# Selective scan of a four-layer sequence kernel: readout through TensorE turns, one scan per state, du*B on GpSimd

## The chip, the cores and the metric

The kernel runs on one core of one Trainium2 chip. The core's engines that matter here are TensorE (PE; its weight loads are shown apart as PEld), VectorE (DVE), ScalarE (ACT), GpSimd (POOL) and SyncE (SP, which issues the DMAs). Each engine works through its own instructions in a fixed order and waits for others by semaphores. SBUF is the working memory; PSUM is the memory that TensorE writes; the kernel lays it out as eight banks of 128 x 512 float32. The metric is device time in microseconds, the median of repeated runs. All tensors here are float32 unless said otherwise.

## The reference: what is computed

A batch of 32 sequences, each 256 tokens by 256 features, passes through four layers: L0 (linear attention with a gated output), L1 (softmax attention with 16 heads), L2 (a two-way selective state-space layer, E = 512 channels, N = 16 states) and L3 (linear attention, 8 heads). The change lies in L2. For each direction, with u the projected input:

```python
dbc = einsum('bse,re->bsr', u, Wdbc)
dlt, Bm, Cm = split(dbc, [R, R + N])
delta = softplus(einsum('bsr,er->bse', dlt, Wdt) + bdt)
A = -exp(Alog)
dA = exp(delta[..., None] * A)
dBu = delta[..., None] * Bm[:, :, None, :] * u[..., None]
def step(h, xs):
    h = dA_t * h + dBu_t
    y = einsum('ben,bn->be', h, C_t)
...
return ys + u * Dp
```

So for each of 512 channels and 16 states there is a recurrence over 256 tokens, and the 16 states are then weighted by C (which depends on token and state alone) and summed. The second direction runs over reversed time. The two results are added, multiplied by silu of another projection (`act_mx`), projected back to 256 features and added to the residual with a gate.

## The kernel before, in words

After a preamble that folds the weights, everything is recorded into a `Plan` (class at L108) and written out by `place` (L217). `place` is a list scheduler: it simulates the engines with the costs that `_cost` (L176) gives for each operation, hands out the buffers named in `_BUFFERS` and `_BANKS` (L37 and L48) one after the other, and picks the operation that can start first, with ties settled by program order less a head start called `rush` (L288). Its picks become each engine's instruction order; nothing is reordered afterwards. Because all recorded operations are issued at L342, the profile shows L342 for nearly everything, and groups are told apart by the names of their tiles. Where the planner sees TensorE idle for over 0.7 us it inserts filler matmuls (L302 to L317; tiles `g<-w_wf,ident`). It takes SBUF-only VectorE operations and GpSimd operations as excluding each other (`_locks`, L207). The helper `together` (L128) records several matmuls as one operation with the sum of their costs.

One batch's work is `front` (L0, L1 and the first part of L2; L965), `project` for two directions (L998), `act_of` (L1034), four calls of `scan` (L1053), and `back` (L1114: the projection back and L3). In the main loop at L1138 the next batch's front and the last batch's back are woven between the steps of `scan`. So a steady stretch of the program repeats once per batch.

`scan(b, d, cp)` works on one direction d and one half cp of the channels: two blocks (c) of 128 channels on the partitions, 256 tokens along the free axis. `du` (delta times u) is made in PSUM (L1058 to L1065). Then, for each of 8 pairs of states (L1076):

- SP broadcasts the pair's rows of B (`bb`) and C (`cc`) from a DRAM tile `cd` to all partitions, 256 KB each;
- ScalarE makes `dA` = exp(delta*A), four instructions of 255 tokens, into SBUF; a zero column before each segment starts the recurrence anew;
- VectorE multiplies `dbu` = du*B, 128x1024, into two PSUM banks (L1090);
- VectorE scans all four segments (2 blocks x 2 states) in one instruction of 1024 elements into `h` (L1096, L1098);
- GpSimd multiplies `h` by `cc` in place (128x1024, L1102) and adds the pair's two states (128x512, L1105);
- TensorE adds the sum to the running output `yp` in PSUM by a matmul with the identity (128x512, L1108).

`yp` began with the u*Dp projection (L1066 to L1074). At the end of direction 1, VectorE multiplies `yp` with `act` (L1112). Channels lie on the partitions throughout, as `back` needs for its projection (`tok_proj` with `act` as the stationary operand).

In all there are 32 x 4 x 8 = 1024 such steps, 32 per batch. PSUM holds `dbu` (2 banks), `du` (1), `yp` (1) and four general banks `g`.

Of the kernel before, what the change touches and what calls it, by code (L numbers as in the profile page):

```python
# [28 lines left out]
for _n, _w in _COLS:  # L29
# [8 lines left out]
    ("x", 1, [P, 2, D]), ("x1", 1, [P, 2, D]), ("x2", 2, [P, 2, D]), ("xs", 1, [P, 2, D]), ("gate", 2, [P, D]),  # L38
    ("xT2", 2, [P, 2, S]), ("dl", 6, [P, 2, S]), ("dbc", 2, [R + 1 + 2 * N, S]),
    ("bb", 3, [P, 2, S]), ("cc", 4, [P, 2, S]), ("dA", 3, [P, 1025]), ("h", 4, [P, 2, 2, S]), ("act", 4, [P, 2, S]),  # L40
    ("qa", 1, [P, 4, S]), ("ka", 1, [P, 4, S]), ("va", 1, [P, 2, 16, 32]), ("ex", 4, [P, 2, S]), ("mT", 1, [16, S]),
# [5 lines left out]
]  # L47
_BANKS = [("dbu", 1, [P, 2, 2, S]), ("du", 1, [P, 2, S]), ("yp", 1, [P, 2, S]), ("g", 4, [P, 512])]  # L48
_IN_BANKS = {name for name, _, _ in _BANKS}

_RUSH = {"du": 500}


_ADDED = (0, 1, 2, 3, 4, 5, 6, 7)
_SPARE = 0.7
# [52 lines left out]
class Plan:  # L108
# [3 lines left out]
    def __init__(self, nc):  # L112
        self.nc = nc
        self.buffers, self.ops, self.filler = {}, [], None
        for name in ("tensor", "vector", "scalar", "gpsimd", "sync"):
            setattr(self, name, Engine(self, name))
# [10 lines left out]

    def together(self, calls, engine="tensor", method="matmul"):  # L128

        self.add(engine, method, [v for args, _ in calls for v in args], {}, calls)  # L130

    def add(self, engine, method, args, kw, calls=None):
        op = Op()
# [17 lines left out]
        if calls:  # L151
            op.cost = sum(_cost(engine, method, views[3 * i : 3 * i + 3])[0] for i in range(len(calls)))
            if engine == "scalar":

                op.cost += 2.5
        op.rush = max(_RUSH.get(v.tile.name, 0) if w else 0 for v, w in views if isinstance(v, View))
        op.locks = _locks(engine, method, views)
# [18 lines left out]
def _cost(engine, method, views):  # L176

    tiles = [(v, w) for v, w in views if isinstance(v, View)]
    n = max([_elements(v) for v, w in tiles if w] or [0])
    if engine == "sync":  # L180
        return 0.06, 2.6
    if engine == "tensor":
        if method == "transpose":
            return 0.3, 0.2
        w = views[1][0]
        if (w.ap if isinstance(w, View) else w).dtype == BF16:
            return max(0.15, 0.17 + n / 2350), 0.2

        if w.shape[0] <= 32:
            return 0.2, 0.2  # L190
        if w.shape[1] <= 32:
            return 0.23, 0.2
        return max(0.27, 0.06 + n / 570), 0.2
    if engine == "scalar":
        ptr = sum(1 for v, _ in views if not isinstance(v, (View, float, int)) and getattr(v, "shape", (0, 0))[1:] == (1,))
        return 0.2 + n / 1400 + 0.05 * ptr, 0.1
    n = max(_elements(v) for v, _ in tiles)
    if engine == "gpsimd":
        if method == "tensor_tensor":
            return (0.7 if n < 8 else 0.12 + n * 0.00223), 0.1  # L200
        return 0.2 + n / 1000, 0.1
    if method == "tensor_tensor_scan":
        return 0.15 + n / 480, 0.08
    return 0.1 + n / 940, 0.08

# [141 lines left out]
def cond_seq_kernel(ctx: ExitStack, tc: tile.TileContext, a: dict, out: bass.AP):  # L347
# [12 lines left out]
    def load(name, shape, src, eng=None, pool=None, **kw):  # L360
        t = (pool or const).tile(shape, kw.pop("dtype", F32), name=name, **kw)
        (eng or nc.sync).dma_start(out=t, in_=src)
        return t
# [20 lines left out]
    wfo = wtile("wf", 4, 256)  # L384
    blocks = load("blocks", [P, 2, P], a["blocks"])
    w0 = {n: wtile(n + "0", 2, 256) for n in ("wk", "wv", "wq")}
    w3 = {n: wtile(n + "3", 2, 256) for n in ("wk", "wv", "wq")}
# [268 lines left out]

    for t in q.buffers["dA"]:
        nc.gpsimd.memset(t[:, 0:1025:256], 0.0)
    for t in q.buffers["va"]:
# [198 lines left out]
    def attention(ch, x, b, dst):  # L858
# [31 lines left out]
        for h2 in range(8):  # L890
# [3 lines left out]
            for t in range(2):  # L894
                for i in range(2):
# [4 lines left out]
                    ))  # L900
            q.together(calls)
            for i in range(2):
# [13 lines left out]
        for g2 in range(2):  # L916
            av = None
            for h4 in range(4):
# [3 lines left out]
                for m in range(2):  # L922
                    for i in range(2):
# [4 lines left out]
                        ))  # L928
                q.together(calls)
                exs = [q.tile("ex") for _ in range(2)]  # L930
# [5 lines left out]
                for m in range(2):  # L936
                    for i in range(2):
# [7 lines left out]
                        ))  # L945
                q.together(calls)
                yield
# [50 lines left out]
    def project(b, d):  # L998
# [9 lines left out]
        cd = q.tile("cd")  # L1008
        q.sync.dma_start(out=cd, in_=dbc[R + 1 :, :])
        yield  # L1010

# [18 lines left out]
        yield  # L1030
        state[b][d] = (cd, dl)
        yield

    def act_of(b):  # L1034

        xT = state[b]["xT"]
        act = [q.tile("act") for _ in range(2)]
        for e2 in range(2):
            ps = bank()
            for j in range(2):  # L1040
                e = 2 * e2 + j
                for k in range(2):
                    q.tensor.matmul(
                        ps[:, j * 256 : (j + 1) * 256], wx[:, k, e * P : (e + 1) * P], xT[:, k, :],
                        start=k == 0, stop=k == 1,
                    )
            dst = flat(act[e2])
            q.scalar.activation(dst, ps, AF.Tanh, bias=0.0, scale=0.5)
            q.vector.scalar_tensor_tensor(dst, dst, 1.0, ps, ALU.add, ALU.mult)
            yield  # L1050
        state[b]["act"] = act

    def scan(b, d, cp):  # L1053

        s = state[b]
        cd, dl = s[d]
        dl = dl[cp]
        du = q.tile("du")  # L1058
        for c in range(2):
            e = 2 * cp + c  # L1060
            for k in range(2):
                q.tensor.matmul(
                    du[:, c, :], wcz[d][:, k, e * P : (e + 1) * P], s["xT"][:, k, :], start=k == 0, stop=k == 1
                )
        q.vector.tensor_tensor(du, du, dl, ALU.mult)  # L1065
        if d == 0:  # L1066
            s["yp"] = yp = q.tile("yp")
            for c in range(2):
                e = 2 * cp + c
                for k in range(2):  # L1070
                    q.tensor.matmul(
                        yp[:, c, :], wdp[:, k, e * P : (e + 1) * P], s["xT"][:, k, :],
                        start=c == 0 and k == 0, stop=False,
                    )  # L1074
        yp = s["yp"]
        for k in range(N // 2):  # L1076
            n = slice(2 * k, 2 * k + 2)
            bb, cc = q.tile("bb"), q.tile("cc")
            q.sync.dma_start(out=bb, in_=cd[N + 2 * k : N + 2 * k + 2, :].partition_broadcast(P))
            q.sync.dma_start(out=cc, in_=cd[n, :].partition_broadcast(P))  # L1080
            dA = q.tile("dA")
            for c in range(2):
                for j in range(2):
                    o = (2 * c + j) * S + 1
                    q.scalar.activation(
                        dA[:, o : o + S - 1], dl[:, c, 1 - d : S - d], AF.Exp, bias=0.0,
                        scale=aneg[d][:, 2 * cp + c, 2 * k + j : 2 * k + j + 1],
                    )
            dbu = q.tile("dbu")
            q.vector.tensor_tensor(  # L1090
                dbu, du.unsqueeze(2).to_broadcast([P, 2, 2, S]), bb.unsqueeze(1).to_broadcast([P, 2, 2, S]), ALU.mult
            )
            h = q.tile("h")
            hf, uf = h.rearrange("p c n s -> p (c n s)"), dbu.rearrange("p c n s -> p (c n s)")
            if d == 0:
                q.vector.tensor_tensor_scan(hf, dA[:, 0:1024], uf, 0.0, ALU.mult, ALU.add)  # L1096
            else:
                q.vector.tensor_tensor_scan(  # L1098
                    hf[:, ::-1], dA[:, 1:1025][:, ::-1], uf[:, ::-1], 0.0, ALU.mult, ALU.add
                )  # L1100
            hn = h.rearrange("p c n s -> p c (n s)")
            q.gpsimd.tensor_tensor(hn, hn, flat(cc).unsqueeze(1).to_broadcast([P, 2, 2 * S]), ALU.mult)  # L1102
            last = d == 1 and k == N // 2 - 1
            if k in _ADDED:
                q.gpsimd.tensor_tensor(h[:, :, 0, :], h[:, :, 0, :], h[:, :, 1, :], ALU.add)  # L1105
            else:
                q.tensor.matmul(yp, ident, h[:, :, 1, :], start=False, stop=False)
            q.tensor.matmul(yp, ident, h[:, :, 0, :], start=False, stop=last)  # L1108
            yield
        if d == 1:  # L1110
            y = s["act"][cp]
            q.vector.tensor_tensor(y, yp, y, ALU.mult)  # L1112

    def back(b):  # L1114

        s = state.pop(b)
        ps = tok_proj(s["act"], wfo, 2, nk=4)
        x3 = q.tile("x3")
# [122 lines left out]
```

## Time and profile before

| What | Value |
|---|---|
| median of 3 runs | 5332.26 us (5331.7 to 5333.14) |
| profiled execution: span | 5331.4 us |
| mean granted TensorE clock | 0.943 |
| busy: PE, PEld | 4592.1 us (86%), 2963.3 us (56%) |
| busy: DVE | 4786.2 us (90%) |
| busy: ACT | 2940.9 us (55%) |
| busy: POOL | 4419.3 us (83%) |
| DMA | 574.36 MB, mean 108 GB/s |
| first scan starts, last scan ends | 249.6 us, 5291.3 us |

The span is that of one execution, from its first to its last instruction; it stands 0.9 us under the median of the runs. The first 250 us are the weight preamble and the first batch's front; from then on the scans of one batch follow those of the last at a steady pace until 5291 us, and the last batch's back takes the final 40 us. A row of a group reads: line, engine, operation, written tile <- read tiles, shapes, count | busy us in all, mean ns of one | idle time of the engine before it and what ended it. A float32 matmul shows as two records, so counts of matmuls are twice those in the code, except for turns (`g<-ident,...`, transposes by a matmul against the identity), which show as one. In a matmul's row `a*b` is rows times columns of the stationary operand.

### The profile page before, as it was taken

The page shows a single profiled execution, that of the slowest core. Times are in us where ns is not written, and L with a number is a line of the kernel's source. Part 1 is how long each engine was busy: PE and PEld are TensorE (multiplying, and loading weights), DVE is VectorE, ACT ScalarE, POOL GpSimd, SP SyncE. Part 2 cuts the span into 40 slices and gives each one's busy share as a digit, 9 for nine tenths or more (in the row PEclk, how much of TensorE's full clock was granted, in tenths as well). Part 3 has the DMA queues.
Part 4 walks back from the last instruction along what each step waited for, and adds up shares of the span by engine and source line. Part 5 has one row for each costly group of instructions (what it writes and reads, how often), then busy time and mean ns, then how long its engine had stood idle before and what let it go on. Part 6 is the DMA issues. An engine that isn't in the chain of part 4 may idle for free. (4 is left out here: it accounts for less than half of the span.)

```text
span 5331.4 us, 65606 instructions
## 1 busy us (share of the span) xinstructions
PE 4592.1 (86%) x20746; PEld 2963.3 (56%) x20746; DVE 4786.2 (90%) x5047; ACT 2940.9 (55%) x6465; POOL 4419.3 (83%) x3487
## 2 busy tenths in 40 slices
PE   6888888888888888888888888888888888888887
PEld 4655555555555555555555555555555555555555
DVE  2399999999999999999999999999999999999997
ACT  1355565555555565656555656555555555555553
POOL 0288898888898888889888889888889888889887
PEclk7899999999999999999999999999999999999999
DMA  3033333333333333333333334333333333333333
GB/s 100 30 115 109 108 116 107 113 111 109 109 113 111 108 112 111 109 109 114 109 111 107 113 106 117 109 112 110 109 109 115 108 111 111 108 110 114 108 112 88
DMA packets 327816, 574.36 MB, mean 108 GB/s; under 512 B 38214, under 2 KB 61066, under 8 KB 327467
## 3 DMA queue, kind: packets, MB, share of 16 engines
q1 hardware_dynamic: 320466, 562.78, 36.1%
q10 hardware_dynamic: 7002, 7.39, 0.4%
q8 instruction: 163, 2.67, 0.2%
q14 instruction: 185, 1.52, 0.1%
HBM read 558.98 MB, written 10.52 MB: 107 GB/s over the span
## 5 line engine op out<-in xcount | busy, mean ns | idle before, releaser
L342 POOL TENSOR_TENSOR h<-h,cc 128x1024 f32<-128x1024 f32 x1024 | 2416.2, 2360 | 502.9 <-issue 384.2
L342 ACT ACTIVATE dA<-dl,alog 128x255 f32<-128x255 f32 x4096 | 1762.0, 499 | 1269.1 <-DVE h L342 1208.2
L342 DVE TENSOR_TENSOR_SCAN h<-dA,dbu 128x1024 f32<-128x1024 f32 x1024 | 2337.8, 2283 | 131.3 <-PE yp L342 33.8
L342 POOL TENSOR_TENSOR h<-h 128x512 f32<-128x512 f32 x1024 | 1301.4, 1271 | 60.8
L342 PE MATMUL yp<-h,ident 128*128 128x512 f32 x2048 | 1154.4, 652 | 201.7 <-POOL h L342 196.5
L342 DVE TENSOR_TENSOR dbu<-du,bb 128x1024 f32<-128x1024 f32 x1024 | 1255.1, 1226 | 20.0
L342 PEld LDWEIGHTS yp<-h,ident 128*128 128x128 f32 x2048 | 344.1, 198 | 511.2 <-POOL h L342 403.6
L342 PE MATMUL g<-w_wf,ident 128*128 128x256 f32 x1756 | 420.8, 382 | 13.6 <-DVE wf L342 13.1
L342 PEld LDWEIGHTS g<-w_wf,ident 128*128 128x128 f32 x1756 | 329.2, 191 | 140.1 <-issue 43.9
L342 ACT ACTIVATE ex<-g 128x512 f32<-128x512 f32 x512 | 273.8, 595 | 147.4 <-PE g L342 139.5
L342 DVE TENSOR_REDUCE mx<-g 128x2 f32<-128x512 f32 x512 | 319.5, 681 | 22.6 <-PE g L342 16.5
L342 PE MATMUL g<-ka,qa 17*128 17x256 f32 x2048 | 334.9, 454 | 1.7 <-DVE mx L342 1.7
L342 PEld LDWEIGHTS g<-ka,qa 17*128 17x128 f32 x2048 | 225.1, 206 | 132.4 <-DVE mx L342 36.5
L342 PE MATMUL g<-ex,va 128*32 128x256 f32 x2048 | 254.4, 386 | 21.0 <-ACT ex L342 21.0
L342 PE MATMUL du<-xT,w_wcz 128*128 128x256 f32 x1024 | 252.0, 389 | 17.1 <-DVE dbu L342 16.3
L342 PE MATMUL g<-ident,wf 128*128 128x128 f32 x768 | 140.2, 292 | 135.7 <-POOL wf L342 132.4
L342 PE MATMUL g<-qa,ka 18*128 18x256 f32 x2048 | 254.7, 401 | 0.7 <-ACT ex L342 0.7
L342 PEld LDWEIGHTS g<-qa,ka 18*128 18x128 f32 x2048 | 155.2, 184 | 145.4 <-issue 112.3
L342 PEld LDWEIGHTS du<-xT,w_wcz 128*128 128x128 f32 x1024 | 188.9, 192 | 72.0 <-DVE dbu L342 35.7
L342 PEld LDWEIGHTS g<-ident,wf 128*128 128x128 f32 x768 | 91.1, 143 | 229.3 <-POOL wf L342 193.2
L342 PE MATMUL yp<-xT,w_wdp 128*128 128x256 f32 x512 | 195.7, 549 | 24.7 <-DVE act L342 24.6
L342 PE MATMUL g<-wf,w_wk 128*128 128x256 f32 x768 | 206.7, 425 | 1.5 <-ACT wf L342 1.4
(236 smaller groups left out, 6232.3 us busy)
## 6 DMA issues: line engine op xcount, KB each, us to landing
bb<-cd SPq DMA_DIRECT2D x1024, 256.0 KB
cc<-cd SPq DMA_DIRECT2D x1024, 256.0 KB
x<-in_x_dram SPq DMA_DIRECT2D x32, 256.0 KB
out_dram<-xo SPq DMA_DIRECT2D x32, 256.0 KB
fw<-in_film_dram SPq DMA_DIRECT2D x3, 1024.0 KB
rwc<-in_wc_dram ACTq DMA_DIRECT2D x2, 1024.0 KB
qa<-mT SPq DMA_DIRECT2D x128, 4.0 KB
cd<-dbc SPq DMA_DIRECT2D x64, 32.0 KB
```

What stands on the lines that cost most here:

```text
L342: getattr(getattr(nc, op.engine), op.name)(*[real(v) for v in args], **{k: real(v) for k, v in kw.items()})
```

## The change

The recurrence and the sums are the same, but the work is cut and laid out differently. Per batch there are still 32 steps; a step is now one block of 128 channels and four states n = 4x + g (x = 0..3) for a fixed g.

- `bb` holds four rows of B (512 KB); `cc` is gone. `du` moves to SBUF (its matmul goes to a `g` bank, `zp`), and GpSimd makes `dbu` = du*B, 128x1024, in SBUF.
- ScalarE writes exp(delta*A) into PSUM, two states (128x512) to a bank; there are two such banks. Each exp has 256 tokens now.
- VectorE runs one scan of 256 elements per state: first operand in PSUM, second in SBUF, result in SBUF with the states innermost (`h` is [128, 256 tokens, 4 states], so a scan writes every fourth float).
- TensorE turns `h` by eight 128x128 transposes into two `g` banks: the partitions become 32 tokens x 4 states, the free axis channels. ScalarE copies each bank (128x512) into `hT`.
- After two blocks c, eight matmuls with stationary operands of 128x32 (`cm`: C on a diagonal pattern that sums the four states of each token) and 256 moving columns add into `yp`, four of them side by side in the four column groups of 32, recorded with `together`. `yp` and `act` have tokens on the partitions now; `act_of` is written accordingly, and `back` turns `act` back with eight transposes and two copies.
- `cm` is made once per `project`: a DMA reads C back from `cd`, GpSimd reorders it, TensorE turns it, ScalarE copies it, and GpSimd expands it (128x1024).
- PSUM: `dA` 2 banks, `yp` 1, `g` 5. The planner's costs are new too: a transpose 0.112 us (0.3 before), float32 matmuls, ScalarE and VectorE entries changed by little, `together` takes a `share` that divides its cost, and `rush` is 400 for the operations that make `du`.

```diff
-    ("bb", 3, [P, 2, S]), ("cc", 4, [P, 2, S]), ("dA", 3, [P, 1025]), ("h", 4, [P, 2, 2, S]), ("act", 4, [P, 2, S]),
+    ("cm", 3, [P, 32, 32]), ("bb", 3, [P, 4, S]), ("dbu", 2, [P, 4, S]), ("h", 2, [P, S, 4]), ("hT", 3, [P, 4, 2, P]),
+    ("du", 2, [P, 2, S]), ("act", 2, [P, 2, E]),
...
-_BANKS = [("dbu", 1, [P, 2, 2, S]), ("du", 1, [P, 2, S]), ("yp", 1, [P, 2, S]), ("g", 4, [P, 512])]
+_BANKS = [("dA", 2, [P, 2, S]), ("yp", 1, [P, 2, S]), ("g", 5, [P, 512])]
...
         if method == "transpose":
-            return 0.3, 0.2
+            return 0.112, 0.25
...
+        return max(0.22, 0.01 + n / 600), 0.25
...
+        cr, cp, ct, cm = (q.tile(n) for n in ("cr", "cp", "ct", "cm"))
+        q.sync.dma_start(out=cr, in_=cd[0:N, :].rearrange("(x g) (q s) -> (g q) x s", x=4, s=32))
+        q.gpsimd.tensor_copy(cp, cr.rearrange("p x s -> p s x"))
+        ps = bank()
+        q.tensor.transpose(ps[:, :32], cp.rearrange("p s x -> p (s x)"), ident[:32, :32])
+        q.scalar.copy(ct, ps[:, :32])
+        q.gpsimd.tensor_tensor(
+            cm, fours.unsqueeze(1).to_broadcast([P, 32, 32]), ct.unsqueeze(2).to_broadcast([P, 32, 32]), ALU.mult
+        )
...
+        for g in range(4):
+            bb = q.tile("bb")
+            q.sync.dma_start(out=bb, in_=cd[N + g : 2 * N : 4, :].partition_broadcast(P))
+            hT = [q.tile("hT") for _ in range(2)]
+            for c in range(2):
+                dbu, h = q.tile("dbu"), q.tile("h")
+                q.gpsimd.tensor_tensor(dbu, du[:, c : c + 1, :].to_broadcast([P, 4, S]), bb, ALU.mult)
+                for m in range(2):
+                    dA = q.tile("dA")
+                    for j in range(2):
+                        n = 4 * (2 * m + j) + g
+                        q.scalar.activation(
+                            dA[:, j, :], dl[:, c, :], AF.Exp, bias=0.0, scale=aneg[d][:, 2 * cp + c, n : n + 1]
+                        )
+                    for j in range(2):
+                        hv, av, uv = h[:, :, 2 * m + j], dA[:, j, :], dbu[:, 2 * m + j, :]
+                        if d == 1:
+                            hv, av, uv = (v[:, ::-1] for v in (hv, av, uv))
+                        q.vector.tensor_tensor_scan(hv, av, uv, 0.0, ALU.mult, ALU.add)
+                for t in range(2):
+                    ps = bank()
+                    for i in range(4):
+                        q.tensor.transpose(
+                            ps[:, i * P : (i + 1) * P], flat(h)[:, (4 * t + i) * P : (4 * t + i + 1) * P], ident
+                        )
+                    q.scalar.copy(hT[t][:, :, c, :], ps.rearrange("p (i e) -> p i e", i=4))
+                yield
+            for t in range(2):
+                calls = []
+                for i in range(4):
+                    calls.append((
+                        (yp[32 * i : 32 * i + 32, t, :], cm[:, 8 * g + 4 * t + i, :], flat(hT[t][:, i])),
+                        {"start": False, "stop": d == 1 and g == 3 and t == 1},
+                    ))
+                q.together(calls, share=4)
...
+                    q.tensor.transpose(ps[:, o : o + P], act[:, t, e * P : (e + 1) * P], ident)
+            yt.append(copy_of(ps, work("b", e2)))
```

## The prediction

> **What bounds the kernel now.** First the page's busy table, then one long steady stretch in the windows view, because the first 250 us (preamble, first front) and the last 40 us hold no scans.
>
> ```profile
> PE 4592.1 (86%) x20746; PEld 2963.3 (56%) x20746; DVE 4786.2 (90%) x5047; ACT 2940.9 (55%) x6465; POOL 4419.3 (83%) x3487
> ```
> ```profile
> core 0: us, PE busy (x) PEld busy (x) DVE busy (x) ACT busy (x) POOL busy (x), PEclk, DMA share, GB/s
> 1035.00:4052.00 3017.00, 2627.42 (x11933) 1685.70 (x11934) 2819.18 (x2928) 1737.01 (x3822) 2620.09 (x2054) 0.95 0.38 110
> ```
>
> That stretch runs from the first scan of one batch to that of another 19 batches later. Per batch the busy times are DVE 148.4, POOL 137.9, PE 138.3, ACT 91.4 us. The scans of the 32nd batch begin at 5162.4, so a batch takes (5162.4 - 249.6) / 31 = 158.5 us: 1.068 times DVE's work. VectorE bounds it, POOL is next. The waits say the same: ScalarE spends its idle time waiting for VectorE.
>
> ```profile
> ACT dA L342 <- DVE h L342: 1208.2, 612, 7.2
> ```
>
> (Who waits for whom: us, times, longest.) So the change is costed per batch on each engine; the largest sum times 1.068 is the new period.
>
> The rows that price it, from the groups (whole run, then two of the steady stretch):
>
> ```profile
> L342 POOL TENSOR_TENSOR h<-h,cc 128x1024 f32<-128x1024 f32 x1024 | 2416.2, 2360 | 502.9 <-issue 384.2 <-PE yp L342 78.5 <-DVE h L342 28.1
> L342 DVE TENSOR_TENSOR_SCAN h<-dA,dbu 128x1024 f32<-128x1024 f32 x1024 | 2337.8, 2283 | 131.3 <-PE yp L342 33.8 <-PE g L342 3.9 <-ACT dA L342 2.4
> L342 POOL TENSOR_TENSOR h<-h 128x512 f32<-128x512 f32 x1024 | 1301.4, 1271 | 60.8
> L342 DVE TENSOR_TENSOR dbu<-du,bb 128x1024 f32<-128x1024 f32 x1024 | 1255.1, 1226 | 20.0
> ...
> L342 DVE TENSOR_TENSOR du<-du,dl 128x512 f32<-128x512 f32 x128 | 88.3, 690 | 19.5 <-PE du L342 16.6
> ...
> L342 ACT COPY wf<-g 128x512 f32<-128x512 f32 x192 | 112.9, 588 | 133.7 <-PE g L342 133.7
> ```
> ```profile
> L342 PE MATMUL yp<-h,ident 128*128 128x512 f32 x1217 | 684.4, 650 | 106.8 <-POOL h L342 103.4
> L342 PE MATMUL g<-w_wf,ident 128*128 128x256 f32 x874 | 209.3, 381 | 8.3 <-DVE wf L342 8.3
> ```
>
> And from the timeline (start, length, ...), for what one instruction costs when the next follows closely:
>
> ```profile
> 2501.25 0.69 DVE L342 TENSOR_TENSOR du<-du,dl 128x512 f32<-128x512 f32 x1
> 2501.85 0.68 DVE L342 TENSOR_TENSOR wf<-g,qm 128x512 f32<-128x512 f32 x1
> 2502.45 1.22 DVE L342 TENSOR_TENSOR dbu<-du,bb 128x1024 f32<-128x1024 f32 x1
> ...
> 2503.09 0.75 PEld L342 LDWEIGHTS g<-ident,wf 128*128 128x128 f32 x7 [0.42 <-POOL wf L342]
> 2503.58 0.68 DVE L342 TENSOR_REDUCE km<-g 128x2 f32<-128x512 f32 x1
> ...
> 2509.18 2.29 DVE L342 TENSOR_TENSOR_SCAN h<-dA,dbu 128x1024 f32<-128x1024 f32 x1
> ```
> ```profile
> 2089.32 1.13 PE L342 MATMUL g<-qa,ka 18*128 18x256 f32 x8
> 2090.38 1.06 PE L342 MATMUL g<-ex,va 128*32 128x256 f32 x8
> 2091.37 1.13 PE L342 MATMUL yp<-h,ident 128*128 128x512 f32 x2
> ```
>
> **VectorE.** Gone: 32 products and 32 long scans. Neighbours on VectorE overlap by 0.08 to 0.09 us (0.69 long, the next 0.60 later; dbu 1.22, the next 1.13 later), so a product takes 1.14 and a scan 2.20 us: 32 x 3.34 = 106.9. Added: 128 scans of 256. The products of 512 and 1024 elements (690, 1226 ns) give 1.047 ns per element and 154 ns fixed; with the same fixed part the scan runs at (2283 - 154) / 1024 = 2.079 ns per element, so 256 take 532 + 154 = 686 ns, and 0.606 us with the overlap. 128 x 0.606 = 77.6 (87.8 with no overlap, 68.1 with no fixed part). Sum 148.4 - 106.9 + 77.6 = **119** us, ends 110 and 129.
>
> No row shows a scan that writes every fourth float. I take the same pace: the scan already spends two elements' time (2 x 1.047) on each, room for a slower store. [...]
>
> **ScalarE.** The exps stay: 128, one token longer. Into PSUM instead of SBUF: between -4 us (the nearest pair, tanh into PSUM 602 and exp into SBUF 631 ns, on 128) and nothing; I take nothing. Added: 64 copies of 128x512 out of PSUM. Alone 588 ns; two such exps of 595 in a row take 1.08 us, so 0.485 each in a row. 64 x 0.485 = 31.0 (37.6 alone), plus two copies in `back` and two small ones, 1.8. Sum 91.4 + 32.8 = **124** us, ends 120 and 131.
>
> **GpSimd.** dbu has the form of the h*cc product it replaces, 2360 ns. The add goes, 1301.4 / 32 = 40.7. `cm` adds two products of 2.36 and two copies under 0.6 (half-size scalings take 571). 137.9 - 40.7 + 5.9 = **103** us.
>
> **TensorE.** Gone: yp, 684.4 / 19 = 36.0, and fillers, 209.3 / 19 = 11.0 (with PE loaded the planner has no gaps to fill). Left: 91.3. Added:
> - 256 turns. Seven loads for turns take 0.75 us, 0.107 each: 27.4. Were each group of four alone, at the 0.60 us that four took with their tail, 38.4.
> - 128 matmuls of 128x32 in 32 groups of four. The ex,va group is the same shape, four matmuls (eight records), but two column groups: the next matmul starts 0.99 us later. Four side by side need half, 0.50, at best; if only two run at once, 0.99. I take 0.50, since the two groups of a step pair follow each other and share the change of shape: 16.0, end 31.7.
> - eight turns in `back`, 0.9.
>
> Sum 91.3 + 27.4 + 16.0 + 0.9 = **136** us, ends 136 and 162. It may fall to 130 where the 91.3 holds tails that denser work covers (a lone turn counts 0.29 us, not 0.107).
>
> [...] The trace grants 0.95 with 54 turns per batch. At half clock the added turns would cost 55 and the sum 163.
>
> **DMA and SP.** `cc` goes and `bb` doubles, half the bytes at a share of 0.38: no bound. The C read-back waits on SP until `cd` has landed, with `bb` loads queued behind; SP's longest wait for that landing in the stretch was 1.1 us, 64 x 1.1 = 70 us at worst. Three `bb` buffers, two steps each, hide it; so nothing.
>
> **New waits.** Turns wait for the last of a step's four scans; all of PE's queue stands behind them, and `hT`, the C matmuls and the layers' matmuls wait for that. ScalarE's copies wait for the turns, with the next exps behind them; only two `dA` banks (1.2 us of scans each) shield VectorE. The planner's order decides how often. I price this by the old ratio 1.068, for want of a nearer row.
>
> **Sum.** TensorE becomes the bound: 135.6 x 1.068 = 144.8 us per batch. 249.6 + 31 x 144.8 + 128.9 x 144.8 / 158.5 (the last batch's scans) + 40 = 4896 us of span. Adding the 0.9 us by which the span lies under the median: **4897 us**, 8.2% faster. With unknown costs at their gentle and harsh ends but groups four wide, PE is 130 to 147, the time 4710 to 5280.
>
> **Rivals.**
> - *Easy packing (0.12).* TensorE's tails vanish (130) and ScalarE's 124 binds as much; ratio near 1.0: 130 per batch, 4430 to 4720. For it: PE's rows are full of tails. Against: in-order queues coupled in a ring.
> - *The shallow buffers bind (0.15).* Three engines within 15% of each other, with two `dA` banks and two `h`, reach 85% where one bound engine reached 94%: 135.6 / 0.85 = 160, 5370; at 0.88, 154, 5190. So 5190 to 5340, about no gain. For it: ScalarE works in blocks (1.08 us for a pair of attention exps, log tables between). Against: the planner knows these costs.
> - *Slower: the column groups run two at a time (0.11).* Price 0.49 us for each of 32 groups, PE 151.3, period 161.6, time about 5430. Decides from PE x 1.068 = 158.5, that is PE 148.4, or 0.90 us per group. For it: the trace shows no four at once. Against: it shows two at once without loss.
> - *Slower: the strided store (0.05).* If a scan takes two more element times for each token, 0.53 us each, VectorE has 187 us and the time is some 6600. Decides at VectorE 148.4, 0.84 us per scan.
>
> The forecast itself has 0.57, for 4720 to 5190.
>
> **Chances.** Differences under 0.2% (11 us) can't be told from no change. Slower: 0.11 + 0.05 and 0.02 of the shallow buffers, 0.18; same 0.02; faster 0.80. The range 4500 to 5350 leaves out the last two rivals and the edge of the first.
>
> **What would show it.** Right: the period near 145; scans near 0.61 us apart and 690 ns long; turns at 0.11 us in a row; a C group in 0.5 us; copies 485 to 590 ns; PE the engine with least idle time. Wrong: C groups near 1 us, scans over 0.84, a granted clock under 0.9, or VectorE idle behind `dA` with TensorE idle too (the shallow buffers).

## The result, and the profile after

The changed kernel takes 5691.9 us (median of 4 runs, 5671.1 to 5716.8), the one before 5332.7 us in the same session: a ratio of 1.0675, 95% interval 1.0642 to 1.0707. It is slower by 359 us; I had predicted 4897.

The page of the changed kernel first: the busy table, then groups (busy us in all, mean ns of one | idle time before them and what ended it). The line number is now L335.

```profile
PE 5052.0 (89%) x34310; PEld 3563.2 (62%) x34310; DVE 3750.0 (66%) x7096; ACT 4101.7 (72%) x8641; POOL 3297.3 (58%) x2588
...
L335 POOL TENSOR_TENSOR dbu<-du,bb 128x1024 f32<-128x1024 f32 x1024 | 2420.0, 2370 | 1303.5 <-DVE h L335 686.7
L335 DVE TENSOR_TENSOR_SCAN h<-dA,dbu 128x256 f32<-128x256 f32 x4096 | 2537.8, 674 | 945.3 <-ACT dA L335 443.2
L335 ACT ACTIVATE dA<-dl,alog 128x256 f32<-128x256 f32 x4096 | 1924.7, 480 | 418.0 <-DVE h L335 356.5
L335 PE MATMUL g<-ident,h 128*128 128x128 f32 x8192 | 1206.1, 286 | 234.4 <-DVE h L335 189.9
L335 ACT COPY hT<-g 128x512 f32<-128x512 f32 x2048 | 1106.7, 586 | 410.5 <-PE g L335 396.4
...
L335 PE MATMUL yp<-hT,cm 128*32 128x256 f32 x8192 | 618.3, 402 | 68.1 <-ACT hT L335 65.3
...
L335 PE MATMUL g<-w_wf,ident 128*128 128x256 f32 x920 | 242.6, 395 | 0.8 <-ACT hT L335 0.5
```

Three of the four engines have about the work that I had costed; TensorE has more. In the steady stretch (all batches but the first and the last) a batch holds 116.0 us of VectorE (predicted 119), 127.7 of ScalarE (124), 102.8 of GpSimd (103) and 153.1 of TensorE (136). But the first scans of two batches are 170.8 us apart in the mean (predicted 144.8). Over a whole batch no engine is busy for more than nine tenths of the period, and all of them stand in each other's idle columns: VectorE waits for ScalarE's exps, ScalarE for VectorE's scans and TensorE's turns, TensorE for scans, GpSimd for scans. The waits view (who waits for whom: us, times, longest) shows the same ring:

```profile
POOL dbu L335 <- DVE h L335: 686.7, 293, 13.0
...
DVE h L335 <- ACT dA L335: 443.2, 443, 4.6
ACT hT L335 <- PE g L335: 396.4, 250, 9.2
ACT dA L335 <- DVE h L335: 356.5, 348, 6.2
...
DVE h L335 <- PE g L335: 255.0, 33, 8.5
```

The last line, where the trace names a turn as what released the scan, is the wait that two `h` buffers make: a scan may not write into `h` until the turns have read it. There are 33 of them, up to 8.5 us each; in nearly every batch it is one wait of about 8.2 us, ahead of the 15th of the 32 steps.

The windows view, one batch per row from first scan to first scan, shows something else. The columns are the busy times of the engines, then the granted clock of TensorE.

```profile
core 0: us, PE busy (x) PEld busy (x) DVE busy (x) ACT busy (x) POOL busy (x), PEclk, DMA share, GB/s
...
1100.03:1280.20 180.17, 161.54 (x1056) 111.93 (x1055) 115.96 (x218) 127.70 (x270) 102.76 (x81) 0.90 0.20 51
1280.20:1447.93 167.73, 149.13 (x1056) 105.30 (x1055) 115.90 (x218) 127.73 (x270) 102.83 (x81) 0.97 0.22 55
```

The same instructions in the same order take 180.2 us in one batch and 167.7 in the next. Only TensorE's busy time differs, with its clock. The clock records hold spells at half clock in multiples of 3.4 us, 601 us in all after the first 260 us; a line through the batches (all but the first and the last) gives 163.0 us plus 0.44 us for each us at half clock (correlation 1.00; 18.8 us per batch in the mean, from 7 to 41). Below, "at full clock" is the intercept of such a line for the kernel at hand: the period that it gives for a batch with no half clock. For the kernel before it is 154.6 us (0.26 us per us, correlation 0.72, 16.4 us per batch); that line is loose, because its batches all hold between 14 and 21 us of half clock.

The means over a batch also hide that its parts have different limits. Here is the second of these two batches cut further, first its steps 9 to 14, then its last eleven steps:

```profile
1319.44:1374.15 54.71, 53.74 (x377) 35.96 (x376) 29.09 (x57) 32.05 (x67) 18.06 (x12) 0.94 0.17 45
1410.74:1447.93 37.19, 32.38 (x254) 23.95 (x251) 30.60 (x52) 34.11 (x77) 29.34 (x16) 0.97 0.35 86
```

The next batch's softmax attention (scores, exps, `ex,va`) lies in the first of the two. There TensorE is busy for 53.7 of 54.7 us and is the bound by itself, and the long wait for turns falls at its end. In the last eleven steps ScalarE is busiest, at 0.92.

### The profile page after: what moved, and what is told of

The parts are those of the page before. It is cut to its first block, busy times and chain, and to the rows that moved or that the text cites. A ratio compares the mean times of both kernels' runs of the same rounds, so it can differ in the third digit from the quotient of the medians.

```text
span 5701.4 us, 92620 instructions
## 1 busy us (share of the span) xinstructions
PE 5052.0 (89%) x34310; PEld 3563.2 (62%) x34310; DVE 3750.0 (66%) x7096; ACT 4101.7 (72%) x8641; POOL 3297.3 (58%) x2588
## 5 line engine op out<-in xcount | busy, mean ns | idle before, releaser
L335 POOL TENSOR_TENSOR dbu<-du,bb 128x1024 f32<-128x1024 f32 x1024 | 2420.0, 2370 | 1303.5 <-DVE h L335 686.7
L335 DVE TENSOR_TENSOR_SCAN h<-dA,dbu 128x256 f32<-128x256 f32 x4096 | 2537.8, 674 | 945.3 <-ACT dA L335 443.2
L335 ACT ACTIVATE dA<-dl,alog 128x256 f32<-128x256 f32 x4096 | 1924.7, 480 | 418.0 <-DVE h L335 356.5
L335 PE MATMUL g<-ident,h 128*128 128x128 f32 x8192 | 1206.1, 286 | 234.4 <-DVE h L335 189.9
L335 ACT COPY hT<-g 128x512 f32<-128x512 f32 x2048 | 1106.7, 586 | 410.5 <-PE g L335 396.4
L335 PEld LDWEIGHTS g<-ident,h 128*128 128x128 f32 x8192 | 952.7, 146 | 569.9 <-DVE h L335 273.9
L335 PE MATMUL yp<-hT,cm 128*32 128x256 f32 x8192 | 618.3, 402 | 68.1 <-ACT hT L335 65.3
L335 DVE TENSOR_REDUCE mx<-g 128x2 f32<-128x512 f32 x512 | 323.3, 686 | 271.5 <-PE g L335 271.2
L335 POOL TENSOR_SCALAR rs<-mv 128x2 f32<-128x2 f32 x256 | 57.4, 224 | 762.7 <-DVE mv L335 757.3
L335 ACT ACTIVATE ex<-g 128x512 f32<-128x512 f32 x512 | 277.7, 594 | 264.8 <-PE g L335 257.1
L335 PEld LDWEIGHTS yp<-hT,cm 128*32 128x32 f32 x8192 | 181.7, 110 | 354.4 <-ACT hT L335 210.8
L335 PE MATMUL g<-ka,qa 17*128 17x256 f32 x2048 | 326.3, 463 | 2.8 <-DVE mx L335 0.5
L335 PE MATMUL g<-qa,ka 18*128 18x256 f32 x2048 | 318.3, 437 | 0.3 <-ACT ex L335 0.3
L335 PE MATMUL g<-ex,va 128*32 128x256 f32 x2048 | 293.7, 416 | 0.0
L335 PEld LDWEIGHTS g<-ka,qa 17*128 17x128 f32 x2048 | 201.4, 212 | 110.1 <-DVE mx L335 61.0
L335 PEld LDWEIGHTS g<-qa,ka 18*128 18x128 f32 x2048 | 189.9, 202 | 125.2 <-issue 97.8
L335 PE MATMUL g<-xT,w_wcz 128*128 128x256 f32 x1024 | 255.2, 394 | 1.6 <-ACT hT L335 1.6
L335 PE MATMUL g<-w_wf,ident 128*128 128x256 f32 x920 | 242.6, 395 | 0.8 <-ACT hT L335 0.5
L335 PEld LDWEIGHTS g<-xT,w_wcz 128*128 128x128 f32 x1024 | 197.0, 200 | 41.1 <-issue 14.7
L335 PEld LDWEIGHTS g<-w_wf,ident 128*128 128x128 f32 x920 | 168.8, 193 | 61.6 <-issue 26.0
L335 POOL TENSOR_TENSOR rs<-rs,nhalf 128x2 f32<-128x2 f32 x256 | 181.8, 710 | 18.8
L335 PEld LDWEIGHTS g<-ex,va 128*32 128x32 f32 x2048 | 102.0, 115 | 134.4 <-issue 77.4
```

Source lines behind the costliest of these rows:

```text
L335: getattr(getattr(nc, op.engine), op.name)(*[real(v) for v in args], **{k: real(v) for k, v in kw.items()})
```

## Experiments

Two theories at the start. **A**: TensorE, busy 153 of 171 us, is the bound all through the batch. **B**: the engines are tied into a ring by two `h` and two `dA` buffers, so that the fixed order can't absorb any delay. All kernels start from the changed one; ratios are to the kernel before.

| Run | us (median) | ratio, 95% interval | half clock, us | period | at full clock |
|---|---|---|---|---|---|
| changed kernel | 5691.9 | 1.0675 (1.0642 to 1.0707) | 601 | 170.8 | 163.0 |
| e1 no fillers | 5690.3 | 1.0666 (1.0650 to 1.0682) | 834 | 170.3 | 161.8 |
| e2 C cut | 5521.4 | 1.0360 (1.0340 to 1.0380) | 617 | 165.3 | 160.5 |
| e3 exps cut | 5416.3 | 1.0152 (1.0135 to 1.0169) | 378 | 162.5 | 157.3 |
| e4 four `h` | 5255.3 | 0.9858 (0.9823 to 0.9894) | 392 | 157.6 | 152.3 |
| e5 control | 5479.6 | 1.0279 (1.0264 to 1.0295) | 205 | 164.1 | 162.0 |
| e6 four `h`, C cut | 5336.3 | 1.0011 (1.0002 to 1.0021) | 989 | 159.3 | 149.0 |
| e7 four `h`, exps cut | 5160.5 | 0.9687 (0.9645 to 0.9728) | 332 | 153.6 | 149.1 |
| e8 `dA` in SBUF | 6652.8 | 1.2472 (1.2453 to 1.2491) | 1560 | 200.8 | 191.7 |
| e9 eight extra matmuls | 5632.4 | 1.0562 (1.0546 to 1.0578) | 143 | 168.7 | 167.3 |
| e10 four `h`, eight extra | 5331.6 | 0.9999 (0.9989 to 1.0008) | 146 | 159.1 | 157.6 |
| e11 scans cut | 5457.8 | 1.0227 (1.0210 to 1.0244) | 371 | 163.6 | 158.4 |
| e12 three `h` | 5434.4 | 1.0190 (1.0145 to 1.0235) | 485 | 162.6 | 156.0 |
| e13 four `h`, one extra | 5185.0 | 0.9720 (0.9704 to 0.9737) | 156 | 154.4 | 152.3 |
| e14 four `h`, two extra | 5215.1 | 0.9777 (0.9762 to 0.9791) | 174 | 155.2 | 152.9 |
| e15 four `h`, three `dA` | 5474.1 | 1.0265 (1.0244 to 1.0286) | 570 | 163.6 | 156.2 |
| e16 all three cuts | 5147.1 | 0.9650 (0.9635 to 0.9664) | 550 | 153.9 | 146.9 |
| e17 four `h`, all three cuts | 5121.7 | 0.9597 (0.9581 to 0.9613) | 798 | 152.9 | not told |

The last three columns are of the profiled run. The fits of e8, e9 and e16 are loose (correlation 0.65 to 0.73), as is that of the kernel before: little varies between their batches. In e17 (0.17) the fit tells nothing.

**e1: fillers left out.**

```diff
-                order.append(fill)
```

> The 920 filler matmuls (busy 242.6 us in all, 7.6 per batch) are left out; the order of everything else stays. Theory A (TensorE binds: 153 of 171 us per batch busy): up to 240 us come back, 5450 to 5550, unless the granted clock falls below the 0.94 of the changed kernel. Theory B (TensorE has slack at these places and the period is set by the ring VectorE - TensorE - ScalarE over two h buffers): the fillers stand in real gaps, 5650 to 5700, no difference over 0.5%. If the clock falls and the turns lengthen, slower than 5700.

Nothing gained, as B said: the fillers stand in gaps (1.2 us per batch at full clock). But the half clock rose from 601 to 834 us, so they also hold the clock up in part.

**e2: C matmuls cut.** Seven of eight C groups are recorded, ordered and then not issued (`op.skip`).

```diff
+                q.skip = g < 3 or t == 0
                 q.together(calls, share=4)
+                q.skip = False
...
-        for args, kw in op.calls:
+        for args, kw in [] if op.skip else op.calls:
```

> Left out: seven of every eight groups of the C matmuls (the sum over states is then incomplete); order, turns and copies stay. This takes 7/8 of 19.3 us, 17 us, from TensorE in each batch. Theory A (TensorE binds): 17 x 1.1 x 31 = 580 us, about 5100. Theory B (the ring over h, which ends at the turn and the copy and does not hold the C matmuls): less than 200 us, 5500 or more.

170 us instead of 580. TensorE's busy time fell by 15.5 us per batch and the period by 5.6 (2.5 at full clock). Theory A falls as the bound of the whole batch. That TensorE binds in the attention stretch alone stays possible: only 48 of a batch's 256 C records (the rows `yp<-hT,cm`) lie in the stretch shown above.

**e3: second exp of each bank cut** (`q.skip = j == 1` around the exp).

> Left out: the second exp of every dA bank (its scan reads a constant 0.5 instead); the rest and the order stay. ScalarE loses 64 of 128 exps, 64 x about 0.5 = 32 us per batch, down to 96; no second exp waits for the first one in its bank. Theory A (TensorE binds): less than 150 us, over 5540. Theory B (ScalarE's copies of turns and exps lie in the ring): 300 us or more, under 5400.

276 us, just short of B's 300: ScalarE lost 27 us per batch, the period 8.3 (5.7 at full clock).

**e4: four `h` buffers.**

```diff
-    ("cm", 3, [P, 32, 32]), ("bb", 3, [P, 4, S]), ("dbu", 2, [P, 4, S]), ("h", 2, [P, S, 4]), ("hT", 3, [P, 4, 2, P]),
+    ("cm", 2, [P, 32, 32]), ("bb", 2, [P, 4, S]), ("dbu", 2, [P, 4, S]), ("h", 4, [P, S, 4]), ("hT", 3, [P, 4, 2, P]),
```

> Four h buffers instead of two, paid by two instead of three for cm and for bb; the order is planned anew by the same planner. All work stays. Theory A (TensorE binds): within 100 us of 5692, over 5590. Theory B (two h buffers tie VectorE's scans to the turns of the step before the last): 8 to 12 us per batch, 250 to 370 us, 5320 to 5440, with VectorE's wait for PE and ScalarE at the scans (443 + 255 us) and POOL's wait for h (687 us) smaller.

437 us less, with the same work: more than B had expected, and 1.4% faster than the kernel before. Its waits view:

```profile
POOL dbu L335 <- DVE h L335: 572.1, 374, 18.1
...
DVE h L335 <- ACT dA L335: 355.7, 411, 3.8
ACT dA L335 <- DVE h L335: 239.0, 382, 2.8
...
PE g L335 <- DVE h L335: 83.6, 142, 1.3
```

The scans' wait for turns is nearly gone (8.2 us in all, instead of 255.0), and ScalarE's longest wait for a scan went from 6.2 to 2.8 us. Is it all depth?

**e5: the control**, `cm` and `bb` two as in e4, `h` two.

> Control for the four h buffers: only what paid for them (cm and bb two instead of three), h stays at two; the same planner plans anew. If the 437 us of the run with four h buffers come from the h buffers: 5640 to 5780, about the changed kernel's 5692. If they come from a new order that happens to fit: under 5500.

5480, the figure of my second case, but not for its reason: at full clock the new order gains 1.0 us per batch, and most of the rest is the clock (205 instead of 601 us at half clock: 396 x 0.44 = 174 of the 212 us). So the depth of `h`, with the order that the planner makes for it, is 162.0 against 152.3, 9.7 us per batch, 300 us.

**e6 and e7: the cuts of e2 and e3 in the order of e4.**

> With four h buffers, and in its order, seven of eight groups of C matmuls are left out (the sum over states is incomplete). TensorE is busy 144.5 of the 157.5 us period there. If TensorE has become the bound: 17 us less per batch, 300 to 550 us below 5255, 4700 to 4950. If the engines still wait for each other in a ring: about the 170 us that the same cut gave with two h buffers, 5050 to 5120.

> With four h buffers, and in its order, the second exp of every dA bank is left out (its scan reads a constant 0.5). ScalarE, busy 126 of 157.5 us, loses about 32. If TensorE alone is the bound: within 80 us of 5255. If the ring through ScalarE still sets the period: 200 to 300 us less, as with two h buffers (276), 4950 to 5050.

e6 is 81 us *slower* than e4 though it does less, which neither reading allowed for. At full clock it would gain 3.3 us per batch, but the half clock went from 392 to 989 us: the C matmuls hold the clock up in this kernel (in e2, with two `h`, the same cut left it at 617). e7 gains 95 us, between my two cases. From here on the clock was a third cause, **C**.

What goes with it can be counted. I cut the traces of nine kernels (changed, e1 to e7, e12) into the windows of 3.41 us in which the clock steps, took those at full clock that hold only turns and matmuls of 128x32 (C and `ex,va`; "C records", two for each matmul), and asked whether the next window was at half clock:

```
turns in the window    under 8 C records    8 or more C records
 0 to  3               104 of 104 low       3 of   4 low
 4 to  7                51 of  51           0 of  63
 8 to 11                54 of  61           2 of 167
12 to 15                 2 of  71           0 of  89
16 or more               0 of 240           0 of 294
```

So of these windows those with 12 or more turns were followed by full clock in 692 of 694 cases, and those with 0 to 7 turns and under 8 C records by half clock in 155 of 155. No run varied the turns alone. The attention's score groups (`g<-ka,qa`, 17 of 128 rows) go with half clock too: in the changed kernel, of the windows without a full-sized matmul and with 20 or more of their records, 22 of 23 were followed by half clock, though TensorE counts as busy for 98% of such a window in the mean. In the kernel before it is 29 of 29. In other orders the share is lower: in e4 it is 9 of 24, and the 15 that kept the clock all held eight turns as well, the 9 none; in e5 it is 1 of 14 and in e12 4 of 31, where most of those that kept it held 8 or 12 C records and at most one turn. So no count of score records alone decides, and what does is open.

**e8: `dA` back in SBUF**, with three `h`, two `cm` and `bb`, seven `g` banks, and the planner told that a scan excludes no GpSimd operation.

```diff
-_BANKS = [("dA", 2, [P, 2, S]), ("yp", 1, [P, 2, S]), ("g", 5, [P, 512])]
+_BANKS = [("yp", 1, [P, 2, S]), ("g", 7, [P, 512])]
...
-    return method not in ("bn_stats", "bn_aggr", "tensor_reduce", "reciprocal")
+    return method not in ("tensor_tensor_scan", "bn_stats", "bn_aggr", "tensor_reduce", "reciprocal")
```

> Undoes one part: the exps go into SBUF (two dA tiles), h has three buffers, cm and bb two, the two PSUM banks go to g (seven); planned anew. If the wait of the second exp of a PSUM bank (510 against 410 ns) matters: exps 0.41 us apart, ScalarE 6 us less per batch, 5050 to 5200. If not, or if three instead of four h buffers cost as much: 5230 to 5400. If a scan that reads only SBUF gets in GpSimd's way, as the planner holds for other VectorE work: scans over 690 ns or dbu over 2400 ns and over 5400.

The third case, far beyond its figure. Its groups, then its timeline (start, length, ...):

```profile
L335 DVE TENSOR_TENSOR_SCAN h<-dA,dbu 128x256 f32<-128x256 f32 x4096 | 3981.6, 1032 | 651.5 <-POOL dbu L335 327.4
L335 POOL TENSOR_TENSOR dbu<-du,bb 128x1024 f32<-128x1024 f32 x1024 | 2547.5, 2492 | 1875.8 <-DVE h L335 1370.0
```
```profile
2505.45 1.71 ACT L335 ACTIVATE dA<-dl,alog 128x256 f32<-128x256 f32 x4
...
2506.01 5.54 DVE L335 TENSOR_TENSOR_SCAN h<-dA,dbu 128x256 f32<-128x256 f32 x5 [1.61 <-ACT dA L335]
...
2507.19 2.65 POOL L335 TENSOR_TENSOR dbu<-du,bb 128x1024 f32<-128x1024 f32 x1 [0.63 <-DVE h L335]
```

Five scans beside a GpSimd product take 5.54 us; a pair in the changed kernel takes 1.26. Scans that overlap no `dbu` product of GpSimd take 685 ns in the mean, those that overlap one 1804, up to 2897; a `dbu` product takes 2492 ns in the mean, against 2370 in the changed kernel. In the changed kernel, with `dA` in PSUM, the scans take 673 and 674. What holds the scan up beside the product the trace doesn't name. With `dA` in PSUM the overlap costs a scan nothing that shows, so that part of the change lets VectorE and GpSimd run side by side. Four exps in a row take 1.71 us here, 0.41 apart.

**e9 and e10: clock held up by extra matmuls**, in the changed kernel and in e4.

```diff
             q.together(calls, share=2)
+            q.ops[-1].calls = [((pss[0][:, 0:256], ident, wfo[:, 0, :]), {"start": True, "stop": True})] + calls
             for i in range(2):
                 q.vector.tensor_reduce(
```

> The changed kernel in its own order, with one more matmul (128x128 by 256 columns of constants, its result overwritten) ahead of each of the eight score groups per batch that feed the row maxima, where the long spells of half clock begin. Added work: 8 x about 0.43 = 3.4 us of TensorE per batch. Clock theory (over the batches of the changed kernel's trace the batch takes 163.0 us plus 0.44 us for each us at half clock, 18.8 us in the mean): the spells over 10 us go, some 400 of the 601 us at half clock, 100 to 180 us less net, 5510 to 5600. If the clock is only a companion of slow batches: the same or up to 100 us slower, 5690 to 5800.

> The same eight extra matmuls per batch in the kernel with four h buffers, in its order. There a batch takes 152.3 us plus 0.46 us per us at half clock, 12.9 us in the mean, most of it in spells of 17 to 21 us in every third batch. Clock theory: 60 to 150 us less net than 5255, 5100 to 5200. Otherwise 5255 to 5360.

The spells over 10 us went (601 to 143 and 392 to 146 us at half clock), so they come from these stretches, as C has it; but the extra matmuls cost 4.3 (a loose fit) and 5.3 us per batch at full clock, 0.54 and 0.66 each instead of 0.43, so the net is 60 us gained and 76 lost. Both times lie outside what C forecast (e9 between my two cases, e10 in the other case), by the price and not by the mechanism. The price says something else too: here, inside the attention stretch, TensorE's added work was paid in full and more, where e2's C groups, most of them outside it, gave 2.5 for 15.5.

**e11: second scan of each bank cut** (`q.skip = j == 1` around the scan).

> The changed kernel in its order, with the second scan of every dA bank left out (half of the states stay at zero). VectorE loses 64 of 128 scans, 64 x 0.60 = 38 us per batch, down to 78. If TensorE or ScalarE were the bound: nothing, 5600 to 5700. If the engines wait for each other in a ring in which a scan is one of the links, as cuts on TensorE and ScalarE (each 15 to 30 us for 3 to 6 us of period) suggest: 4 to 12 us per batch, 5320 to 5570.

4.6 us at full clock for 35 us less of VectorE, which is busy for two thirds of the time: it is no bound, yet the period depends on it, as B has it.

**e12: three `h` buffers**, `cm` and `bb` two.

> Three h buffers, cm and bb two as in the control and in the run with four. Between 5480 (two) and 5255 (four): if the depth acts step by step, 5330 to 5400; at full clock between 162.0 and 152.3 us per batch.

The time lies above what I expected, because of the clock (485 us); at full clock it is 156.0, between 162.0 and 152.3. The third buffer gives 6.0 us, the fourth 3.7. The sum of the scans' waits for turns doesn't follow this: 202.7 us in e5, 365.5 in e12, 8.2 in e4. Each order spends its waits elsewhere, so the gain can't be read off that one row.

**e13 and e14: one or two extra matmuls** in e4 (`if h2 == 3:`, `if h2 in (2, 5):` ahead of e9's line).

> Four h buffers; one extra matmul per batch instead of eight, ahead of the fourth of the eight score groups, in the middle of the stretch where the spells of 17 to 21 us begin. Eight cost 5.3 us per batch at full clock (157.6 against 152.3), so one about 0.7. If one breaks the chain of low windows: half clock from 392 to about 200 us, 6 us per batch less of it, worth 2.8; net 2 us per batch, about 60 us, 5170 to 5230. If it moves the spells elsewhere: 5240 to 5300.

> Four h buffers; two extra matmuls per batch, ahead of the third and the sixth score group, so that no window of 3.4 us holds three score groups and nothing else. Cost about 1.3 us per batch, gain up to 3.7 (half clock from 12.9 to 4.6 us per batch, as with eight): 5160 to 5220. If two are not enough: 5250 to 5320.

One is enough: 156 us at half clock, no cost that shows at full clock, 5185.0 us. In e4's order, with one matmul more, the half clock per batch falls by 8.1 us (12.9 to 4.8) and the period by 3.2, where the line's 0.46 us per us gives 3.7: the clock is a cause of the time and no mere companion. e13 beats the kernel before (0.9720, 0.9704 to 0.9737) and the changed one by 507 us.

**e15: three `dA` banks** (`g` four), in e4.

> Four h buffers and three dA banks instead of two, paid by one of the five banks of g; planned anew. If the two dA banks are what holds the period 7.5 us above the predicted one: at full clock 146 to 150 us per batch, 5050 to 5200. If not, or if the missing bank of g costs as much: 152 to 156, 5250 to 5400.

Slower than either case. At full clock 156.2, 3.9 us worse, with more half clock beside: a third `dA` doesn't pay for a bank of `g`. A third `dA` beside all five banks of `g` would make nine banks, where every kernel here lays PSUM out as eight; it was not tried.

**e16 and e17: all three cuts at once** (C groups, second exps, second scans), with two and with four `h`.

> The changed kernel in its order with all three cuts at once: seven of eight C groups, the second exp and the second scan of every dA bank are left out. Alone they gave 2.5, 5.7 and 4.6 us per batch at full clock. If the period is a chain through the three engines: 12.8 or more, at full clock 150 or less; without the C groups the half clock grows, so 5150 to 5330. If something outside the three holds it (GpSimd, DMA, the layers' own chain of steps): the gains stop near the largest, 156 to 158, 5350 to 5450.

> The same three cuts with four h buffers, in that order; alone C gave 3.3 and the exps 3.2 us per batch at full clock (152.3). Chain: 9 or more, 143 or less, though with 20 to 35 us per batch at half clock, so 4950 to 5150. Something outside: 147 to 149, 5150 to 5280.

e16's time lies 3 us under the range of the chain. Its 146.9 at full clock is a loose figure, for nearly all its batches hold 17.1 us of half clock (one batch fewer at each end, and the line gives 138.7). The period says it without a line: 153.9 against 170.8, 16.9 us less at 17.1 against 18.8 us of half clock per batch, a difference worth 0.7. That is more than the three alone (2.5 + 5.7 + 4.6 = 12.8). So the cuts add up, and no one of the three engines is the bound of the whole batch. A chain through all three does that; so would a batch whose stretches are bound by different engines, as the window rows have it, and these runs don't part the two. e17's 5121.7 lies in the range of the chain, but its value at full clock can't be told. In it the chain of work that ended last can be followed through most of the span; TensorE has nearly half of it, and GpSimd more than ScalarE and VectorE together:

```profile
PE 47%; POOL 18%; ACT 10%; DVE 6%; DMA 5%; issue 4%; POOLq 0%; SPq 0%; DVEq 0%; ACTq 0%
```

With the cuts made, the order with four `h` buffers is worth 25 us; but e17 spends 248 us more at half clock than e16, so this doesn't price the depth.

## Why the prediction was wrong

**VectorE (119) and GpSimd (103)**: right, 116.0 and 102.8. The strided store costs nothing that shows: 674 ns a scan against the 686 that I had worked out, and the rival with it is refuted; the two more element times for each token that it took show in no run.

**ScalarE (124)**: 127.7, within its ends, but by a step that I had the wrong way round. I put the exps into PSUM at between -4 us and nothing, and took nothing. The second exp of a bank starts 512 ns after the first (median), the next bank's first 415 after that; before it was 399. In the timeline of the changed kernel:

```profile
1334.08 1.26 DVE L335 TENSOR_TENSOR_SCAN h<-dA,dbu 128x256 f32<-128x256 f32 x2
...
1349.45 0.97 ACT L335 ACTIVATE dA<-dl,alog 128x256 f32<-128x256 f32 x2
```

Two exps of 0.48 us take 0.97, nothing overlaps; 64 x 0.1 = 6 us per batch. The trace shows what holds the second one: nearly all second exps (1986 of 2048) wait for a semaphore that ScalarE itself raises, and where one follows its first directly it starts 33 ns after that has ended. The first exp of the next bank, which waits for VectorE, starts 62 ns before the end of the exp ahead of it. Whether the chip needs that wait was not tried.

**TensorE (136)**: the terms were too small. Turns 1206.1 / 32 = 37.7 instead of 27.4: nearly the harsh end, "each group of four alone" (38.4). C 19.3 instead of 16.0, 0.60 us for each of the 32 groups, where the rival that they go two at a time needed 0.90 to decide; so that rival fails. Four records start 6 or 7 ns apart, and a group alone takes 0.64 us with its tail:

```profile
1331.07 0.64 PE L335 MATMUL yp<-hT,cm 128*32 128x256 f32 x8
```

The fillers, which I took as gone, stayed with 7.6: a planner's order full of waits has gaps to fill. And part of the busy time is half clock: in e4's batches with little of it TensorE is busy 141.0 of 153.7 us.

```profile
1185.52:1339.25 153.73, 141.01 (x1042) 100.51 (x1041) 116.66 (x219) 125.82 (x270) 102.62 (x81) 0.99 0.23 60
...
1493.35:1656.67 163.32, 149.78 (x1042) 106.83 (x1041) 117.08 (x218) 126.14 (x270) 102.69 (x81) 0.93 0.23 57
```

(Two of its batches, columns as above.) Still, this was not what decided: 15.5 us of TensorE less gave 5.6.

**New waits**, priced "by the old ratio 1.068": **the step that failed.** Measured, the ratio of the period to the largest sum, TensorE's, is 171.3 / 153.1 = 1.12 (all batches but the first and the last). The old ratio belongs to one bound engine with four `h` buffers behind it. Here three engines hand each step on through two `h` buffers, a cut on any of them shortens the period by a fraction of the work cut, and all three cuts add up. The forecast also took one engine as the bound of the whole batch; the window rows show TensorE as the bound in the attention stretch and ScalarE busiest in others. My rival "the shallow buffers bind" names the mechanism, and I gave it 0.15 and 154 to 160 us; it was 163.0 at full clock. Of the two buffers it named, `h` is shown (9.7 us per batch); for `dA` the one run speaks against it, with a bank of `g` less.

**The clock**: I read 0.95 as a property that would stay, and so it nearly did (16.4 us per batch at half clock before, 18.8 after). Turns in a row stand 109 ns apart at full clock and 213 at half clock (medians in the changed kernel), so the doubled cost of a turn that I allowed for at half clock is there, but only 466 of the 8192 turns of `h` start in it. What I missed is the price: a us at half clock costs 0.44 us now. Before, with VectorE the bound, it was 0.26 by the loose line; that it was less is likely, and not shown. Windows full of score groups were followed by half clock in both kernels (22 of 23 and 29 of 29).

**The read-back of C**, costed at nothing: SP's part is small (29.3 us of waits for `cd` in 1870 us of the trace), but the turn of `cp` stands in TensorE's queue and waits for GpSimd: 120.5 us in 62 waits, 3.8 per batch, not priced. No run takes it away.

The miss per batch is 170.8 - 144.8 = 26.0 us. The changed kernel has 7.8 of half clock (170.8 to 163.0), 1.0 for the order that comes with fewer `cm` and `bb` (to 162.0), and 9.7 for the depth of `h` (to 152.3). Not all of the half clock is a miss, for the old ratio had some in it: at full clock it is 154.6 / 148.4 = 1.042 (by the loose line), which would have forecast 141.3. So the forecast held 3.5 us of half clock, 4.3 of the miss are the clock, and 152.3 - 141.3 = 11.0 are left. These I can only argue: with TensorE at 141.0 instead of 135.6 us, e4's ratio of 153.7 / 141.0 = 1.09 gives an estimated 5.9, and some 5 stay open. In the changed kernel the cuts gave 0.13 to 0.21 us at full clock for each us of work, so no single cost explains the rest. Why the planner's order with four buffers is not tighter stays open; its new cost entries, which decide the order (those of the score groups, halved by `share`, among them), were not varied.

## What to carry to other kernels

When a change brings three engines within some 15 to 25 per cent of each other, the sum of the busiest one times the old packing ratio is no forecast; cut the loop into its stretches and look for the bound of each, count the buffers on each hand-over, and treat a step from four to two as a cost of its own. Read the granted clock batch by batch: where the same instructions take 180 and 168 us, the clock is a term of the time, and a removed matmul can take away what held it up (e6: 392 to 989 us at half clock with the C groups cut). One extra matmul at the place where a spell begins was worth far more than it cost (e13: 70 us less than e4); with eight per batch the price ate much of the gain in one kernel (e9: 60 us left) and more than all of it in the other (e10: 76 us lost).

## What the runs showed of the hardware that I had not expected

- Of the windows of 3.41 us at full clock that hold turns and matmuls of 128x32 alone (nine kernels), those with 12 or more 128x128 turns and under four matmuls of 128x32 were followed by full clock in 309 of 311 cases, those with 0 to 7 turns and under four such matmuls in none of 155. With four or more such matmuls beside 4 to 11 turns it was 228 of 230. Windows with 20 or more records of 17-row groups and no full-sized matmul were followed by half clock in 22 of 23 cases in the changed kernel, but in 4 of 31 in e12.
- A scan of 256 with both inputs in SBUF took 685 ns in the mean beside no `dbu` product of GpSimd and 1804 where it overlapped one (e8). With one input in PSUM (the changed kernel): 673 and 674.
- Two exps of ScalarE into the same PSUM bank start 512 ns apart (median), the second behind a semaphore of ScalarE's own in 1986 of 2048 pairs; into the next bank it is 415, into SBUF 399 in the kernel before and about 410 in e8.
- Scans of 256 that write every fourth float took 674 ns in the mean, where I had worked out 686 for dense ones.
